# Four graph layers on one TensorE: a hand-written event list made binding for every engine, a first range without Strassen-style products, and counts split in three

## The chip, the cores and the metric

The kernel runs on one core of a Trainium2 chip. The metric is the device time of one launch in microseconds (us), the median of several runs. One launch computes four layers, whose heavy part is seven multiplications of a 2708 x 2708 adjacency matrix with a feature matrix 512 wide, all in float32.

## The reference, cut to what matters

```python
deg = jnp.maximum((adj != 0).astype(jnp.float32).sum(-1), 1.0)
x = _layernorm(x + _L0_gnn_ref(x, adj))      # inc = adj + (adj > 0) / sqrt(count of adj > 0 in the row)
                                             # (inc @ x) / (row sum of inc)
x = _layernorm(x + _L1_gnn_ref(x, adj, adj, ...))   # adj @ x, then an attention-weighted adj @ (x @ W_sa)
x = _layernorm(x + _L2_gnn_ref(x, adj, weight))     # three hops: p = adj @ p, each through a 512 x 512 weight
x = _layernorm(x + _L3_gnn_ref(x, adj, deg[..., None], W, b))
```

Layer 0 needs, for every row of adj, the number of positive entries (the "count") before its product can start, and the sum of the row of inc afterwards. Layer 1 needs two sweeps over adj (one plain, one with attention weights in place of adj), layer 2 three sweeps, layer 3 one.

## The kernel before, in words

**Sweeps and ranges.** Each of the seven multiplications is a sweep, S[0] to S[6], over four ranges of output rows (`RANGES`, L29: 384, 384, 256 and 330 rows of each half; sweep 0 takes them in the order 256, 384, 384, 330, `RANGES0`, L30). The matrix is cut into halves of NH = 1354: A11, A12, A21, A22 against B11, B12, B21, B22. A range is computed with seven products instead of eight, in the manner of Strassen and Winograd: sums of A tiles (s1 to s4, function `comb`, L246, issued at L269 to L272) and of B tiles (T1 to T4, function `x_sums`, L152) are formed on DVE (VectorE), seven products P1 to P7 run on PE (TensorE, L283), and the results are put together from PSUM (`copy_out` on ACT, L304, and `add` on DVE, L311). A product is 11 row tiles (13 in sweeps 3 to 5) by two column blocks. The profile counts two records per float32 matmul, so that one product of an 11-tile sweep shows 44.

**The event list.** Nothing is written in the order of execution. Every step is put on a list by `at(position, function)` (L115). A position is counted in products: a range is 7 long, a sweep 28. At the end the list is sorted and run (L807). So `at(pb + 6.08, ...)` means "when product 6 of this range has just begun". The functions issue instructions to the framework, which adds the semaphores, gives out buffers and orders the instructions of each engine itself: with a cost model it takes, for every engine, the first instruction in list order that it thinks ready. An instruction later in the list can so be put ahead of an earlier one.

**Buffers.** The tiles of A, the temporaries of sweep 0 ("s") and of sweep 2 ("e", "f"), the loads for counting ("cl"), the rows and running sums share one ring of `RING` = 44 buffers of 128 x 384. `NTMP` = 12 temporaries hold products on their way out, `nat` has 7 tiles of 128 x 512, masks have 3 buffers. All eight PSUM banks share one tag.

**Queues.** A tiles, count tiles and re-read features go through SP's DMA queue (`load` L240, L408, `fetch` L386). B tiles go through POOL's (`x_load` L177), except those that ACT's queue loads at the start. Weights go through ACT's.

**Around the change.**
- *Counts* (sweep 0). `count_tile` (L402) does three things in one event: it loads a tile of adj (L408), makes a 0/1 mask with two ACT instructions, Sign and Relu (L410, L411), and multiplies the mask by a column of ones on PE (L416). `count_row` (L419) turns counts into count^-0.5 (DVE, then POOL's power), spreads it over partitions with PE transposes (L434), and ACT copies it into `row` (L437). For the first range the counts of half 0 use the tiles of A that are loaded anyway; those of half 1 load A21 and A22 a second time as "cl".
- *prep0* (L446). For each tile of A in sweep 0, DVE forms mask times row (L449), adds it (L450), and adds the tile to a running row sum (`add_run`, L444). *prep2* (L634) does the like for the attention weights of sweep 2. `run_sums` (L453) reduces the running sums on PE. Both halves are reduced at position 4.5 of a range.
- *done* functions (L328 to L333) take the finished rows of half 1 at position 6.08 and of half 0 at 7.06, three tiles each: transposes or dense products on PE, a layernorm (L336: DVE statistics, POOL's power at L343, DVE's last step at L345), stores.
- *Order of products*: `PLAIN` (L31) is P1, P7, P5, P6, P2, P4, P3. `FIRST` (L32) is that of the first range of sweep 0. P2 uses A12 against B21; P4 uses A22; P3 uses s4, which `comb` writes over A12.
- *next_x* (L179) loads the B tiles of the next sweep while the last range of this one still runs.

Of the kernel before, what the change touches and what calls it, by code (L numbers as in the profile page):

```python
# [30 lines left out]
PLAIN = dict(P1=0, P7=1, P5=2, P6=3, P2=4, P4=5, P3=6)  # L31
FIRST = dict(P1=0, P2=1, P7=2, P5=3, P6=4, P4=5, P3=6)  # L32
STAT = dict(P1="B11", P7="T3", P5="T1", P6="T2", P2="B21", P4="T4", P3="B22")
MOV = dict(P1="11", P7="s3", P5="21", P6="11", P2="12", P4="22", P3="12")
RING = 44
NTMP = 12
# [7 lines left out]
def gnn_kernel(ctx: ExitStack, tc: tile.TileContext, x, adjT, w_sa, a_sa, w_gcn, b_gcn, wab, bab, w_hop, w_out,  # L44
# [58 lines left out]
    def nat(nm):  # L103
        return pool.tile([P, D], F32, name=nm, tag="nat", bufs=7)

    def mask_tile():
        return pool.tile([P, 384], BF, name="mask", tag="mask", bufs=3)
# [44 lines left out]
    def x_sums(k):  # L152
        w = wt(k)
        b = b12.pop(k)
        b11, b21, b22 = (X[s, k] for s in ("B11", "B21", "B22"))
        for d, i, j in (("T3", b22, b), ("T1", b, b11), ("T2", b22, "T1"), ("T4", b21, "T2")):
            j = X[j, k] if isinstance(j, str) else j
            nc.vector.tensor_tensor(new_x(d, k)[:w], i[:w], j[:w], ALU.subtract)  # L158

    def b12_tile(k):  # L160
        b12[k] = pool.tile([P, HD], F32, name="b12", tag="b12", bufs=3)
        return b12[k]
# [16 lines left out]
    def next_x(base, src, direct, sums=0.95, halves=0.50):  # L179


        for k in range(KT):
# [3 lines left out]
            if not late:  # L186
                at(base - 5.8 + f, lambda k=k: x_load(src, k, "B11", q))
                at(base - 1.8 + f, lambda k=k: x_load(src, k, "B21", q))
                at(base - 0.8 + f, lambda k=k: x_load(src, k, "B22", q))
                at(base - 0.8 + f, lambda k=k: x_load(src, k, "B12", q))  # L190
                at(base - 0.4 + f, lambda k=k: x_sums(k))
# [23 lines left out]
    def sweep(base, nk, ranges, prep=None, extra=None, done=None, evac=None, ext_src=None, lead=0.0, first=False,  # L215
              late=None):
        A, spare = {}, {}
        for r, (R0, n) in enumerate(ranges):
            pb = base + 7 * r
            ph = FIRST if first and r == 0 else PLAIN  # L220
            ks = range(nk)

            def load(ij, k, R0=R0, n=n, r=r, ph=ph):
                hi, hj = int(ij[0]) - 1, int(ij[1]) - 1
                w = wt(k)
                if ph is FIRST and ij == "22" and k >= KT - 8:
# [19 lines left out]
            def comb(dst, a, b, op, k, n=n, r=r):  # L246
# [3 lines left out]
                nc.vector.tensor_tensor(A[r, dst, k][:w, :n], A[r, a, k][:w, :n], A[r, b, k][:w, :n], op)  # L250

            when = {"11": (-1.0, 1.0), "21": (-0.4, 1.0), "22": (0.5, 1.0), "12": (2.4, 1.0)}
            cw = {"s3": 0.3, "s1": 1.1, "s2": 2.1, "s4": 5.05}
            if ph is FIRST:
                when = {"11": (-4.0, 0.2), "12": (-3.8, 0.2), "21": (-0.3, 0.4), "22": (0.2, 0.4)}
# [590 lines left out]
```

## Time and profile before

| | us |
|---|---|
| median of 3 runs (3285.07 to 3288.18) | 3286.8 |
| the profiled execution | 3290.12 |
| its span, first to last instruction | 3288.3 |
| PE busy / its idle time in the span | 3166.4 / 121.9 |
| DVE, ACT, POOL busy | 1648.1, 567.6, 349.1 |
| first product starts / sweep 1's first product starts | 61.06 / 533.96 |

All times after this come from that profiled execution. "Busy" for PE is a modelled, pipelined time: PE that is busy is not always PE at its peak, so a product's length is best read where products follow each other without a break. "The chain of waits" follows the work that ended last back to what released it. "Waits" lists for an engine how long it stood idle before an instruction and which engine released it. A window gives busy times, the granted TensorE clock and the DMA engines' share for a stretch of the span. DMA-issuing instructions are shown on the queue's own row (SPq, ACTq, POOLq) and are not counted as busy.

### The profile page before, as it was taken

How to read it: one execution, taken by the hardware profiler on the slowest of the kernel's cores; microseconds unless marked ns; L12 is line 12 of the kernel's file. 1: busy time of each engine (PE TensorE's matmuls, PEld its weight loads, DVE VectorE, ACT ScalarE, POOL GpSimd, SP SyncE). 2: the span in 40 equal slices, each digit the busy share in tenths (PEclk: the TensorE clock that was granted, in tenths of full speed). 3: DMA queues.
4: the chain of work that ended last, by engine and by line, in shares of the span. 5: the costliest groups of instructions: out<-in, count | busy, mean ns of one | idle time of the engine just before them, and what ended most of it. 6: DMA issues, size and time to landing. Idle time of an engine off the chain costs nothing.

```text
span 3288.3 us, 35613 instructions
## 1 busy us (share of the span) xinstructions
PE 3166.4 (96%) x12046; PEld 2050.3 (62%) x12046; DVE 1648.1 (50%) x4093; ACT 567.6 (17%) x1126; POOL 349.1 (11%) x604
## 2 busy tenths in 40 slices
PE   3998999999999999999999999999999999999998
PEld 2755566556765555764556865568656587655675
DVE  6687687334346865975223333323244243643444
ACT  4432500000025544641000000000000000000000
POOL 2001023000000010113000010000011011300000
PEclk9999998999999999999999999999999999999999
DMA  6665665422434342553432453324444344533340
GB/s 201 205 145 121 169 97 138 93 70 50 93 81 111 100 134 80 147 163 118 108 98 72 121 159 90 108 71 116 130 128 125 89 142 130 179 112 99 108 128 33
DMA packets 268683, 383.21 MB, mean 117 GB/s; under 512 B 35199, under 2 KB 230071, under 8 KB 268500
## 3 DMA queue, kind: packets, MB, share of 16 engines
q1 hardware_dynamic: 231096, 291.61, 34.0%
q0 software_dynamic: 28688, 78.49, 7.6%
q10 hardware_dynamic: 8716, 10.84, 1.1%
q8 instruction: 95, 1.56, 0.2%
q14 instruction: 88, 0.72, 0.1%
HBM read 325.31 MB, written 55.49 MB: 116 GB/s over the span
## 4 chain that ended last, share of the span: by engine, by line
PE 83%; issue 6%; DVE 4%; DMA 4%; POOL 2%; ACT 0%; SPq 0%; POOLq 0%; ACTq 0%; DVEq 0%
PE accu L283 21%; PE accc L283 20%; PE accd L283 20%; PE acca L283 10%; PE ps_d L381 8%; DMA cl<-in_adjT 1%; PE ps_n L367 1%; POOL B L177 1%; POOL rstd L343 1%; DMA a<-in_adjT 1%; PE ps_t L373 1%; PE pz L606 1%; DVE T L158 0%; DVE run L444 0%; DVE s L449 0%
## 5 line engine op out<-in xcount | busy, mean ns | idle before, releaser
L250 DVE TENSOR_TENSOR a<-a,a 128x384 f32<-128x384 f32 (+4 forms) x988 | 485.0, 507 | 260.1 <-DMA a<-in_adjT 107.8
L283 PE MATMUL accu<-a,B 128*128 128x384 f32 (+5 forms) x1232 | 395.1, 464 | 0.0
L283 PE MATMUL accc<-s,T 128*128 128x384 f32 (+5 forms) x1232 | 373.3, 458 | 3.6 <-DVE s L250 3.6
L283 PE MATMUL accd<-a,B 128*128 128x384 f32 (+5 forms) x1232 | 376.4, 451 | 0.0
L283 PE MATMUL acca<-a,B 128*128 128x384 f32 (+5 forms) x1232 | 367.7, 452 | 0.0
L283 PE MATMUL accd<-a,T 128*128 128x384 f32 (+5 forms) x1232 | 364.2, 453 | 0.3 <-DVE a L250 0.3
L283 PE MATMUL accu<-a,T 128*128 128x384 f32 (+5 forms) x1232 | 360.6, 450 | 0.0
L283 PE MATMUL accc<-a,T 128*128 128x384 f32 (+5 forms) x1200 | 354.5, 452 | 0.0
L250 DVE TENSOR_TENSOR s<-a,a 128x384 f32<-128x384 f32 (+4 forms) x332 | 166.8, 506 | 318.2 <-PE accc L283 263.7
L283 PEld LDWEIGHTS accc<-s,T 128*128 128x128 f32 (+1 forms) x1232 | 233.8, 194 | 115.8 <-issue 6.7
L283 PEld LDWEIGHTS accd<-a,T 128*128 128x128 f32 (+1 forms) x1232 | 233.3, 191 | 114.6 <-issue 2.4
L283 PEld LDWEIGHTS accu<-a,B 128*128 128x128 f32 (+1 forms) x1232 | 233.0, 196 | 111.5 <-issue 23.8
L283 PEld LDWEIGHTS accu<-a,T 128*128 128x128 f32 (+1 forms) x1232 | 231.7, 190 | 110.5
L283 PEld LDWEIGHTS accc<-a,T 128*128 128x128 f32 (+1 forms) x1200 | 226.1, 190 | 112.6 <-ACT W L304 2.2
L283 PEld LDWEIGHTS accd<-a,B 128*128 128x128 f32 (+1 forms) x1232 | 226.5, 190 | 106.2 <-issue 13.5
L283 PEld LDWEIGHTS acca<-a,B 128*128 128x128 f32 (+1 forms) x1232 | 228.6, 190 | 102.9
L311 DVE TENSOR_TENSOR W<-W,accd 128x384 f32<-128x384 f32 (+2 forms) x56 | 28.1, 505 | 313.9 <-PE accd L283 311.7
L311 DVE TENSOR_TENSOR W<-W,U 128x384 f32<-128x384 f32 (+2 forms) x56 | 28.3, 509 | 280.2 <-ACT U L304 279.2
L444 DVE TENSOR_TENSOR run<-run,a 128x384 f32<-128x384 f32 (+5 forms) x328 | 165.2, 505 | 0.6
L343 POOL TENSOR_TENSOR rstd<-rstd,neg_half 128x1 f32<-128x1 f32 (+1 forms) x88 | 54.8, 623 | 1039.8 <-DVE rstd L342 1034.0
L304 ACT COPY U<-accu 128x384 f32<-128x384 f32 (+2 forms) x56 | 24.4, 439 | 584.9 <-PE accu L283 583.7
L641 ACT ACTIVATE e<-row,neg_s 128x384 f32<-128x384 f32 (+4 forms) x176 | 100.8, 573 | 96.5 <-DVE a L644 32.1
(178 smaller groups left out, 2997.6 us busy)
## 6 DMA issues: line engine op xcount, KB each, us to landing
a<-in_adjT SPq DMA_DIRECT2D x560, 192.0 KB
a<-in_adjT SPq DMA_DIRECT2D x280, 165.0 KB
a<-in_adjT SPq DMA_DIRECT2D x273, 128.0 KB
cl<-in_adjT SPq DMA_DIRECT2D x80, 192.0 KB
ld<-X SPq DMA_DIRECT2D x60, 256.0 KB
Y<-y POOLq DMA_DIRECT2D x54, 256.0 KB, 2.3
B<-Y POOLq DMA_DIRECT2D x84, 128.0 KB, 3.4
X<-o POOLq DMA_DIRECT2D x36, 256.0 KB, 3.2
```

What stands on the lines that cost most here:

```text
L177: eng.dma_start(out=t[:w], in_=q)
L250: nc.vector.tensor_tensor(A[r, dst, k][:w, :n], A[r, a, k][:w, :n], A[r, b, k][:w, :n], op)
L283: nc.tensor.matmul(B[home, c][:, :n], X[STAT[p], k][:w, c * P : (c + 1) * P], A[r, MOV[p], k][:w, :n], start=bool(start and k == k0), stop ...
L304: nc.scalar.copy(T[nm, c][:, :n], B[home, c][:, :n])
L311: nc.vector.tensor_tensor(d[:, :n], T[t, c][:, :n], o[:, :n], ALU.add)
L343: nc.gpsimd.tensor_tensor(rstd[:w, 1:2], rstd[:w, 0:1], neg_half[:w], ALU.pow)
L367: nc.tensor.transpose(ps[:w, c * P : (c + 1) * P], C[h, c][:, lo : lo + w], ident)
L373: nc.tensor.transpose(ps[:, c, :w], cols(dsts, c)[:w], ident[:w, :w])
L381: nc.tensor.matmul(ps[:w], lhs(c), wts[c], start=c == 0, stop=c == DC - 1)
L444: nc.vector.tensor_tensor(run[R0, h][:w, :n], run[R0, h][:w, :n], t[:w, :n], ALU.add)
L606: nc.tensor.matmul(pz[:w], C[h, c][:, lo : lo + w], wab_sb[:, c, :], start=c == 0, stop=c == DC - 1)
L641: nc.scalar.activation(e[:w, :n], row[R0, h][0][:w, :n], AF.Exp, bias=neg_s[:w, t : t + 1])
```

## The change

It does the following.

1. After the list has run, every instruction is tied to the one before it on its engine, so that each engine's order is the list's.
2. The first range of sweep 0 is computed as eight plain products (A11·B11 + A12·B21 and so on), one position earlier; it needs no sums of A or B. The B sums for the later ranges are made at position 6.0, T3 in the place of B12. The X tiles come through SP and ACT, in an order of their own.
3. Counts are split into `count_load`, `count_mask` and `count_tile`, half a product and a fifth of a product apart; `count_row` is split from `spread_row`. The first range's counts of half 1 take their masks from the loaded A21 and A22, and the masks of half 0 are made on DVE.
4. P4 comes before P2; s4 is written over A11 instead of A12; half 1 is finished from position 5.15 (before: 6.08), half 0 from 7.12 (before: 7.06).
5. Running row sums take s1 and s4 (22 additions per range) instead of the four tiles (44), except in the plain range; `run_sums` of half 0 first adds half 1's.
6. Layernorms in sweep 0, except the last one, take their last step on ACT.
7. Buffers: ring 46, temporaries 9, `nat` 6, masks 4, `b12` 4. Loads of A22 and A12 come later in a range, B21 of the next sweep later too; in sweep 1 mask and count are two events; in sweep 6 two early loads move with the order of products.

```diff
-PLAIN = dict(P1=0, P7=1, P5=2, P6=3, P2=4, P4=5, P3=6)
-FIRST = dict(P1=0, P2=1, P7=2, P5=3, P6=4, P4=5, P3=6)
+PLAIN = dict(P1=0, P7=1, P5=2, P6=3, P4=4, P2=5, P3=6)
+FIRST = [("11", "B11", "a"), ("12", "B21", "a"), ("11", "B12", "b"), ("12", "B22", "b"),
+         ("21", "B11", "c"), ("22", "B21", "c"), ("21", "B12", "d"), ("22", "B22", "d")]
-RING = 44
-NTMP = 12
+RING = 46
+NTMP = 9
...
-                at(base - 1.8 + f, lambda k=k: x_load(src, k, "B21", q))
-                at(base - 0.8 + f, lambda k=k: x_load(src, k, "B22", q))
-                at(base - 0.8 + f, lambda k=k: x_load(src, k, "B12", q))
-                at(base - 0.4 + f, lambda k=k: x_sums(k))
+                at(base - 0.89 + f, lambda k=k: x_load(src, k, "B21", q))
+                at(base - 0.88 + f, lambda k=k: x_load(src, k, "B22", q))
+                at(base - 0.87 + f, lambda k=k: x_load(src, k, "B12", q))
+                at(base - 0.6 + f, lambda k=k: x_sums(k))
...
+                if sums and (dst, a) in (("21", "21"), ("11", "12")):
+                    add_run(R0, int(dst == "21"), n, w, A[r, dst, k])
-            when = {"11": (-1.0, 1.0), "21": (-0.4, 1.0), "22": (0.5, 1.0), "12": (2.4, 1.0)}
-            cw = {"s3": 0.3, "s1": 1.1, "s2": 2.1, "s4": 5.05}
...
+            when = {"11": (-1.0, 1.0), "21": (-0.4, 1.0), "22": (0.75, 0.8), "12": (3.2, 1.0)}
+            cw = {"s3": 0.3, "s1": 1.25, "s2": 2.1, "s4": 4.3}
+            pw = {ij: (p + 0.3, f) for ij, (p, f) in when.items()}
+            if plain:
+                when = {"11": (-4.0, 0.2), "12": (-3.8, 0.2), "21": (-2.4, 0.4), "22": (-1.6, 0.4)}
+                pw = {"11": (-0.9, 0.6), "12": (-0.3, 0.6), "21": (3.3, 0.9), "22": (4.1, 0.9)}
...
+                for i, (home, h, e) in enumerate((("a", 0, 0), ("b", 0, 1), ("c", 1, 0), ("d", 1, 1))):
+                    at(pb + 2 * i + 2.02, lambda a=(home, h, e), f=whole: f(*a))
...
-                p0 = pb + (6.08 if h else 7.06)
+                p0 = pb + (5.15 if h else 7.12) if not plain else pb + (8.12 if h else 4.15)
...
+        if on_scalar:
+            nc.vector.scalar_tensor_tensor(rstd[:w, 0:1], mv[:w, 0:1], -1.0, rstd[:w, 1:2], ALU.mult, ALU.mult)
         for d, c0, c1 in dsts:
+            if on_scalar:
+                nc.scalar.activation(d[:w], y[:w, c0:c1], AF.Identity, bias=rstd[:w, 0:1], scale=rstd[:w, 1:2])
+                continue
...
+    def count_mask(R0, n, h, i, t=None, on_vector=False):
+        w = wt(i % KT)
+        t = cnt.pop((R0, h, i)) if t is None else t
+        cnt[R0, h, i] = m = mask_tile()
+        if on_vector:
+            nc.vector.tensor_scalar(m[:w, :n], t[:w, :n], 0.0, None, ALU.is_gt)
+        else:
+            nc.scalar.activation(m[:w, :n], t[:w, :n], AF.Sign)
+            nc.scalar.activation(m[:w, :n], m[:w, :n], AF.Relu)
...
+            for h, p, d in ((0, -3.7, 0.05), (1, 1.9, 0.055)):
+                for i in range(NT):
+                    a = lambda h=h, i=i: A[0, f"{h + 1}{i // KT + 1}", i % KT]
+                    at(pb + p + d * (i - 2 * h), lambda h=h, i=i, a=a: count_mask(R0, n, h, i, a(), h == 0))
+                    at(pb + p + d * i, lambda h=h, i=i: count_tile(R0, n, h, i))
...
+                    q = pb + p + 2.5 * i / NT
+                    at(q - 0.5, lambda i=i, h=h: count_load(R1, n1, h, i))
+                    at(q - 0.2, lambda i=i, h=h: count_mask(R1, n1, h, i))
+                    at(q, lambda i=i, h=h: count_tile(R1, n1, h, i))
...
-        for h in range(2):
-            at(pb + 4.5 + 0.05 * h, lambda h=h: run_sums(R0, n, h, inverse))
+        at(pb + (5.6 if r else 3.3), lambda: run_sums(R0, n, 0, inverse, r > 0))
+        at(pb + (2.6 if r else 6.4), lambda: run_sums(R0, n, 1, inverse, r > 0))
...
     for k in range(KT):
         f = k / KT
-        at(-3.0 + f, lambda k=k: x_load(X0, k, "B11", nc.scalar))
-        at(-0.8 + f, lambda k=k: x_load(X0, k, "B21", nc.gpsimd))
-        at(-0.2 + f, lambda k=k: x_load(X0, k, "B22", nc.gpsimd))
-        at(0.0 + f, lambda k=k: x_load(X0, k, "B12", nc.gpsimd))
-        at(0.6 + f, lambda k=k: x_sums(k))
-    at(4.0, start0)
+        at(-5.0 + f, lambda k=k: x0_load(k, "B11"))
+        at(-4.5 + 0.3 * f, lambda k=k: x0_load(k, "B21"))
+        at(-4.0 + 0.3 * f, lambda k=k: x0_load(k, "B12"))
+        at(-3.0 + 0.3 * f, lambda k=k: x0_load(k, "B22"))
+        at(6.0 + 0.9 * f, lambda k=k: x_sums(k))
+    at(2.6, start0)
...
-        for ij, p in (("11", -0.6), ("21", 0.05), ("22", 0.9), ("12", 4.1)):
+        for ij, p in (("11", -0.6), ("21", 0.05), ("22", 1.05), ("12", 3.6)):
             for k in range(KT):
                 at(pb + p + 0.8 * k / KT, lambda ij=ij, k=k: go(ij, k))
+                at(pb + p + 0.8 * k / KT + 0.12, lambda ij=ij, k=k: tally(ij, k))
...
-        early = {(1, 2): -2.0, (1, 3): -1.9, (0, 0): -2.0, (0, 1): -1.9}
+        early = {(1, 2): -0.95, (1, 3): -0.9, (0, 0): -1.0, (0, 1): -0.95}
...
     for _, _, fn in sorted(events, key=lambda e: e[:2]):
         fn()
+
+    last = {}
+    for i in nc.cur_bb.bb.instructions:
+        if i.engine in last:
+            tc.add_manual_dep(i, last[i.engine].name,
+                              mybir.DependencyInfo(mybir.DependencyClass.NoSync, mybir.DependencyReason.DATA),
+                              reason="order of the list")
+        last[i.engine] = i
```

In the diff `plain` is true for the first range of sweep 0, where `pb` is -1; `start0`, which loads the attention weights of layer 1 and reduces them on DVE, moves from 4.0 to 2.6.

## The prediction

> **What bounds the kernel now.** I read the page's parts 1 and 2, then PE's waits, then windows cut at the ranges of sweep 0.
>
> ```profile
> PE 3166.4 (96%) x12046; PEld 2050.3 (62%) x12046; DVE 1648.1 (50%) x4093; ACT 567.6 (17%) x1126; POOL 349.1 (11%) x604
> ...
> PE   3998999999999999999999999999999999999998
> ```
>
> PE is the bound: it stands idle for 121.9 us only, and the slices put about half of that in the first 82 us. The rest must be seen in windows (sweep 0's ranges start at 61.06, 151.40, 283.47 and 423.01):
>
> ```profile
> 0.00:61.06 61.06, 10.56 (x93) 6.57 (x93) 29.37 (x92) 31.32 (x90) 20.30 (x41) 1.00 0.85 258
> 61.06:151.40 90.34, 83.71 (x480) 68.78 (x480) 64.59 (x197) 43.51 (x98) 4.59 (x6) 0.96 0.55 165
> 151.40:283.47 132.07, 124.17 (x527) 74.27 (x527) 104.00 (x264) 47.82 (x101) 12.07 (x19) 0.93 0.64 162
> 283.47:423.01 139.54, 125.67 (x555) 76.24 (x554) 105.22 (x273) 45.62 (x102) 17.76 (x29) 0.95 0.60 132
> 423.01:533.96 110.95, 103.63 (x442) 73.24 (x441) 95.69 (x275) 6.12 (x12) 28.48 (x51) 0.95 0.68 140
> ```
>
> The columns are length, then busy us of PE, PEld, DVE, ACT, POOL, then clock, DMA share, GB/s. Before 61.06 PE works 10.6 us, while the DMA engines are 0.85 busy. In the four ranges the clock is 0.93 to 0.96 (1.00 in nearly all of what follows) and DVE is busy 72 to 86% of the time. Who holds PE:
>
> ```profile
> PE cnt L416 <- ACT mask L411: 46.3, 25, 9.3
> ...
> PE ps_t L373 <- DVE o L345: 21.3, 6, 6.4
> PE pr L434 <- POOL r L431: 5.6, 6, 1.2
> ```
>
> The first line is for 0 to 61, the others for 61 to 600. PE waits for the masks of the counts, in front of a product whose operands are ready: it executes its queue in order, and the counts of half 1 stand ahead of P1. Later it waits for layernorms that are late on DVE. After 600 its waits sum to only 17 us, 9.1 of them for the last `add` (U, L311).
>
> **PE's own work.** Without a break, a product takes:
>
> ```profile
> 585.81 14.19 PE accd L283 x44
> ...
> 838.71 9.50 PE accd L283 x44
> ...
> 934.28 12.21 PE accd L283 x44
> ```
>
> for 384, 256 and 330 rows. Beside products: from 356.44 to 372.44 one product with 11 count groups took 16.0, so (16.0-14.19)/11 = 0.17 a group of three; a finished tile 0.44+0.44+0.81 = 1.7 (transposes, transposes, the small product, spacings at 412 to 420); sums and row spreads about 2 a range. Range 1: 99.3 + 44 x 0.17 + 6 x 1.7 + 2 = 118.9. It took 132.1: 13.2 lost. Range 2, likewise: 20.6. Range 3: 85.5+10.2+2.5 = 98.2, 12.8 lost. Range 0 has 66.5+7.5+6.8+1.5 = 82.3, 8.0 lost. Sum 54.6, and 50 before the start.
>
> **The start.** Loads before the first count of range 1 (list position 0.0): X 5.55 MB and range 0 of A 5.55 MB. The 2.8 MB of A21 and A22 read twice for counts are gone. From 2 to 26 us the window shows 298 GB/s at a DMA share of 0.95: 11.1 MB take 37 us, to 39. Then a count tile, a mask (2 x 0.42) and PE: 42. At that point the first product is over (its masks, 22 x 0.29 on DVE, and its rows are ready near 23; preparation is 2 x 0.336 a tile against PE's 0.86). The other end is SP's own issue:
>
> ```profile
> 0.74 17.66 SPq L240 DMA_DIRECT2D a<-in_adjT  x22
> ```
>
> 0.80 each; 77 of them take 62 us, so 64 instead of 42. I take 42, since SP, in a calmer stretch (44.11, two in 0.86), issued one in 0.43. X leaves POOL's queue; POOL has nothing else then. The Trainium skill ("DMA: Bandwidth & Descriptors", "Rules for kernel authors") says that spreading DMAs over SP, ACT and GpSimd brings no bandwidth and saves issue time only; by it, moving X to SP costs nothing up to SP's limit. This change tests that.
>
> **Range 0, plain.** From 0.0: the seven products that remain after the first one (7 x 9.5 = 66.5; the seven of before cost the same, so the added eighth is the one that runs before 42, beside the loads), range 1's counts 7.5, half 1's own counts 2.6 (22 groups of two at 0.12), two finished tiles of half 0 3.4, sums and row spreads 1.5: 81.5. ACT is short here: between positions -0.2 and 2.3 it makes 22 masks of 0.84 and 22 of 0.61 and two copies, 32.6 us, while PE needs 19.6+5.6 = 25.2 for that stretch: +7.4. `start0` waits on its weights, but ACT issues them some 7 us before DVE's next tile is due: 0 (3 if not). Range 1 so starts at 42+81.5+7.4 = 131, against 151.4. DVE saves the 44 sums of A in this range and makes its 44 x_sums at 6.0 instead of before the start (44 x 0.336 = 14.8 us); PE's last two products cover them, and without that cover they would stand before range 1's preparation.
>
> **Ranges 1 to 3.** `add_run` falls from 44 to 22 (22 x 0.47 = 10.3 us of DVE; in sweep 2 too, where PE doesn't wait for it: 0). P4 before P2 lets half 1 be finished at 5.15, and this takes its three layernorms out of the crowded place around 7. What is left there: from 7.02 to the third layernorm, 30 instructions of 0.47 and three layernorms of 3.4 (0.67+0.60+0.12+0.07, POOL's wait 1.8, 0.15), 24.3 us; PE reaches the third transposes 20.4 after the same point: 4 lost a range, 6 in the first (x_sums beside it). The 1.8 is this row, between the statistics and L345:
>
> ```profile
> 308.42 0.55 DVE L345 TENSOR_SCALAR o<-ld,mv,rstd 128x512 f32<-128x512 f32 x1 [1.31 <-POOL rstd L343]
> ```
>
> The last step on ACT has no row; ACT with one scale pointer took 0.72 (L613, 128x512), a bias pointer adds at most 0.13 (L641 0.611 against L304 0.478): 0.72 to 0.85, taken 0.85, against 0.55 on DVE. So the chain to PE gets 0.4 longer and DVE 0.4 shorter. By the skill ("ScalarE: Activation LUTs", "What ACT_TABLE_LOAD costs"), 280 + 0.833 ns per element and 93 for a second pointer, it would be 0.80; the rule speaks against the move, the sum stays within 0.1 us a tile. **New wait:** `run_sums` at 5.6 stands right behind DVE's added addition, which stands behind a layernorm from 5.45: PE waits 1.3 to 2, and products queue behind it. Counts in three steps take off POOL's 5.6 and the mask waits of 5.5: a mask is due 0.2 of a product (2.8 us) before its count, and a count row 0.15 (2.1 us) before its spread, against a chain of 1.75 (last count at 25.18, transposes at 26.94). So ranges 1 to 3: 126, 124, 103 (now 132.1, 139.5, 111.0). Sweep 1 starts at 131+126+124+103 = 484 instead of 534: **-50**.
>
> **Sweeps 1 to 6.** No arithmetic changes on PE. P4 before P2 frees A22 a product earlier and moves half 1's finish under P2; half 0's transposes get 0.06 of a product more (0.9 us): of the 9.1 us of waits for U I give 5 back. B21 is loaded behind P2, 0.3 of a product (4 us) before x_sums, against 3.4 us to landing on POOL's queue; T1 is needed two products later: 0. Smaller pools (9, 6): lifetimes fit, 0. Masks apart from counts in sweep 1: -1. A binding order costs something unknown: nothing if the old order was near the list's, at most about 1 us in each of 24 ranges from rows like `ps_d <- xT` (0.5): 0 to 24, I take 4, the near end, because DVE and ACT are idle over half of these sweeps. The tail behind the last product is unchanged. Net **-2**.
>
> **Sum.** 3290.1 - 52 = 3238 for a profiled execution; that stands 3.3 above the median of before, so 3235 as a median. What a measurement of this kernel tells from no change is about 0.2%, 6.6 us.
>
> **Rivals.**
> 1. *Only the start gains.* Ranges 1 to 3 keep their 46.6 us, because DVE's list still has prep, sums and layernorms in one place. For it: DVE 79, 75 and 86% busy. Against: 10 us less of DVE each, and less at 7. -20 or (SP-bound, half) -10: about 3270.
> 2. *The binding order makes PE slower.* Place: the three or so tiles around 7.1 to 8.2 of every range. A list counted in products knows nothing of transfers and layernorms; one late DMA on SP or a POOL round trip on DVE stops all behind it, and nothing may pass. Price: the 4 us that I find in sweep 0, in the other 24 ranges, 96: 3286.8-52+96 = 3331. It decides from 2.2 us a range. For it: DVE stands 1.8 us in each layernorm, SP waits 639 us for buffers behind `accc`. Against: PE has only 17 us of waits in those sweeps now, and outside sweep 2 the slices show DVE 20 to 60% busy, so a late step there is caught up before PE needs the next one.
> 3. *The order changes nothing* in sweeps 1 to 6, because the framework followed the list already. The time is the forecast's; only the cause differs, so it has no chance of its own; a version with the list order alone, or without it, would tell.
> 4. *More than forecast:* ranges 1 to 3 at PE's floor, ACT no hindrance: -80, 3206.
>
> **Chances.** Forecast (3206 to 3270) 0.62, rival 1 (to 3280) 0.14, below 3206 0.05; within 0.2% 0.04; slower 0.15, rival 2. Faster 0.81. The range 3206 to 3290 leaves out rival 2 and the lowest case, 0.20, and takes in SP's issue end (+22) and the order's (+20).
>
> **What would show it.** First product near 23 to 30, second near 42 (64: SP bound). Range 1 starts near 131; ACT masks lead PE's waits between 42 and 75. `add_run` (L444) with some 180 to 190 records instead of 328. Granted clock in ranges 1 to 3 above 0.96. `ps_t <- DVE`/ACT at most 5 us a range. Sweep 1's first product near 484, and from there to the end the same 2754 us within 15. Wrong if PE's waits after sweep 0 grow beyond 40, or sweep 1 starts after 515.

## The result, and the profile after

The changed kernel takes 3402.8 us (median of 4 runs, 3401.7 to 3405.7), the kernel before 3287.5 (median of 4): a ratio of 1.035, with an interval of 1.0334 to 1.0370. It is slower by 115 us where 52 us less were forecast, and lies above the range and above rival 2's 3331 too. The profiled execution has a span of 3401.5.

The page's parts 1 and 2 of the changed kernel (busy us of each engine; 40 slices of 85 us in tenths, with the granted clock in the last line):

```profile
PE 3201.7 (94%) x12090; PEld 2064.8 (61%) x12090; DVE 1607.5 (47%) x3914; ACT 548.2 (16%) x1092; POOL 323.3 (10%) x571
...
PE   5878986999999899999899999999999999999998
...
PEclk8989998999999999999999999999999999999999
```

PE's idle time has grown from 121.9 to 199.8 us, and its busy time from 3166 to 3202. An eighth product of 9.5 us is in that; the rest goes with a lower clock, in the mean of the span 0.976 instead of 0.987. The first slice is better than before in busy time (5 for 3); slices 2, 3, 6, 7, 14 and 20 are worse, and slices 1 and 3 have a lower clock. Slices 14 and 20 lie in sweep 2 and in sweep 3's first range.

Where that is, the windows cut at the ranges of sweep 0 tell (the columns as before: length, busy us of PE, PEld, DVE, ACT, POOL, clock, DMA share, GB/s):

```profile
0.00:26.48 26.48, 5.38 (x47) 3.18 (x47) 7.81 (x31) 1.66 (x2) 1.43 (x7) 1.00 0.73 213
26.48:161.20 134.72, 100.70 (x577) 81.26 (x578) 76.97 (x221) 63.97 (x146) 7.06 (x11) 0.89 0.60 159
161.20:308.50 147.30, 125.82 (x539) 74.41 (x538) 108.02 (x262) 54.03 (x108) 12.99 (x22) 0.93 0.57 133
308.50:450.10 141.60, 129.67 (x556) 77.93 (x555) 99.92 (x254) 50.60 (x108) 15.58 (x26) 0.94 0.60 127
450.10:595.90 145.80, 110.71 (x439) 75.03 (x437) 94.69 (x258) 7.96 (x15) 30.61 (x56) 0.87 0.61 121
```

The start gained 34.6 us (61.1 to 26.5). Then the four ranges lost 44, 15, 2 and 35, so that sweep 1 starts at 595.9 instead of 534.0. From there on, sweep 1 is 5 shorter, sweep 2 is 57 longer (555.5 for 498.8), sweeps 3 to 5 are together 9 shorter and sweep 6 is 9 longer.

What PE waits for, over the whole span of the changed kernel:

```profile
PE cnt L459 <- ACT mask L449: 45.8, 23, 14.4
PE deg L653 <- DVE mask L641: 28.2, 6, 13.9
PE cnt L459 <- DVE mask L446: 18.1, 18, 3.8
```

Before, all such waits sum to 108 us, now to 188. No single releaser stands out: masks of counts (L446, L449), the masks of sweep 1 (L641), transposed tiles (L407, 13.1), layernorms, running sums. Four places can be read in full.

**Range 0.** In the changed kernel's timeline, ACT's first mask for the next range:

```profile
52.12 0.52 ACT L448 ACTIVATE mask<-cl 128x384 bf16<-128x384 f32 x1 [26.62 <-DMA cl<-in_adjT]
```

PE at the same time:

```profile
53.26 0.24 PE L459 MATMUL cnt<-ones_bf,mask 128*128 128x1 bf16 x3 [14.35 <-ACT mask L449]
```

And SP's queue ahead of it:

```profile
43.35 4.11 SPq L245 DMA_DIRECT2D aw<-in_adjT  x8
47.97 13.37 SPq L438 DMA_DIRECT2D cl<-in_adjT  x18
```

The first product is over at 38.9 (its last group starts at 29.63 and takes 9.27). PE then stands 14.35 us before a count of range 1, though the second product's operands lie ready (DVE prepares the last of its A tiles until 43.1), since the count's tile is issued by SP at 47.97 only, behind all of range 0's tiles and X.

The second longest wait of this range, 7.91 us, is made by the fixed order on ACT. A mask stands there behind the last step of a layernorm (part 6 of the change), which waits for DVE:

```profile
116.83 0.81 ACT L375 ACTIVATE o<-ld,rstd 128x512 f32<-128x512 f32 x1 [12.80 <-DVE rstd L372]
118.67 0.24 PE L459 MATMUL cnt<-ones_bf,mask 128*128 128x1 bf16 x3 [7.91 <-ACT mask L449]
```

In e3 below, where ACT alone is free, masks go ahead of that step, and PE's waits for them behind the second product are at most 1.85 us.

**The end of sweep 0.** DVE in the timeline of the changed kernel:

```profile
573.38 0.43 DVE L161 TENSOR_TENSOR T<-b,B 128x256 f32<-128x256 f32 x1 [12.25 <-DMA b<-X]
```

PE there:

```profile
575.39 0.24 PE L653 MATMUL deg<-ones_bf,mask 128*128 128x1 bf16 x3 [13.87 <-DVE mask L641]
575.49 2.55 PE L288 MATMUL accd<-a,B 128*128 128x330 f32 x4
```

POOL there:

```profile
571.17 0.54 POOL L181 DMA_DIRECT2D B<-X  x1 [5.63 <-DMA SR<-rcol]
```

DVE stands 12.25 us before x_sums of one B tile. The masks of sweep 1 (L641, 574.98) are next in its list, so PE's degree count (13.87) and behind it the rest of P3 stand as well; P3, by the code, holds the B22 buffers that POOL's next loads need, and those loads stand behind small stores of rcol. Further rounds follow (5.13 and 2.79 at DVE, 6.85 and 2.08 at PE). PE's idle time in this range is 35.1 us; before it was 7.3.

**Sweep 2, a product at DVE's pace.** PE's timeline of the changed kernel in P5 of the first range:

```profile
1117.52 1.56 PE L288 MATMUL accd<-a,T 128*128 128x384 f32 x4 [0.56 <-DVE a L255]
1124.52 1.44 PE L508 MATMUL rs<-ones_f,run 128*128 128x1 f32 x6 [5.44 <-DVE run L491]
1125.83 7.09 PE L288 MATMUL accd<-a,T 128*128 128x384 f32 x16
```

DVE's, just before that wait ends:

```profile
1119.04 0.55 DVE L255 TENSOR_TENSOR a<-a,a 128x384 f32<-128x384 f32 x1
1119.62 0.56 DVE L491 TENSOR_TENSOR run<-run,a 128x384 f32<-128x384 f32 x1
1120.10 0.55 DVE L715 TENSOR_TENSOR e<-e,f 74x384 f32<-74x384 f32 x1
1120.74 0.56 DVE L716 SCALAR_TENSOR_TENSOR a<-a,e 74x384 f32<-74x384 f32 x1
```

Per tile DVE makes four instructions in a row (weight, weight, s1, running sum), 2.12 us, while PE uses a tile of P5 up in 1.29. PE's groups of four start 2.12 apart (1115.40, 1117.52); then it waits 5.44 before the reduction of the sum, with four tiles of P5 behind it. P5 takes 25.0 us from its first matmul to its last; before it took 14.9, with 0.64 of P6 in between.

**Sweep 2, the border of two ranges.** PE's transposes wait for a layernorm, as rival 2 has it, in P7 of the second range, which takes 34.1 us from start to start (25.8 in e1 below):

```profile
1248.67 1.11 PE L405 MATMUL ps_t<-ident,ld 128*128 128x128 f32 x4 [2.58 <-DVE ld L377]
```

### The profile page after: what moved, and what is told of

Same layout as the page of the kernel before. It is cut to its first block, busy times and chain, and to the rows that moved or that the text cites. A ratio compares the mean times of both kernels' runs of the same rounds, so it can differ in the third digit from the quotient of the medians.

```text
span 3401.5 us, 35466 instructions
## 1 busy us (share of the span) xinstructions
PE 3201.7 (94%) x12090; PEld 2064.8 (61%) x12090; DVE 1607.5 (47%) x3914; ACT 548.2 (16%) x1092; POOL 323.3 (10%) x571
## 4 chain that ended last, share of the span: by engine, by line
PE 47%; issue 12%; DVE 3%; DMA 2%; POOL 1%; ACT 0%; SPq 0%; ACTq 0%; POOLq 0%; DVEq 0%
PE accu L288 12%; PE accd L288 11%; PE accc L288 11%; PE acca L288 6%; PE ps_d L413 6%; DMA x3T<-X3T 1%; DMA b<-Y 1%; PE ps_n L399 1%; DVE a L255 0%; PE ps_t L405 0%; DVE run L491 0%; DVE e L715 0%; POOL B L181 0%; POOL Y L389 0%; DMA b<-X 0%
## 5 line engine op out<-in xcount | busy, mean ns | idle before, releaser
L255 DVE TENSOR_TENSOR a<-a,a 128x384 f32<-128x384 f32 (+5 forms) x963 | 433.8, 505 | 118.1 <-DMA a<-in_adjT 117.8
L288 PE MATMUL accu<-a,B 128*128 128x384 f32 (+5 forms) x1188 | 379.9, 466 | 1.3 <-DVE a L497 1.3
L288 PE MATMUL accd<-a,B 128*128 128x384 f32 (+5 forms) x1188 | 359.1, 457 | 0.0
L288 PE MATMUL accu<-a,T 128*128 128x384 f32 (+5 forms) x1188 | 349.7, 452 | 0.0
L288 PEld LDWEIGHTS accu<-a,B 128*128 128x128 f32 (+1 forms) x1188 | 224.4, 195 | 113.2 <-issue 22.5
L288 PEld LDWEIGHTS accc<-s,T 128*128 128x128 f32 (+1 forms) x1188 | 225.5, 195 | 110.6 <-issue 10.0
L288 PEld LDWEIGHTS accu<-a,T 128*128 128x128 f32 (+1 forms) x1188 | 223.5, 190 | 109.6
L288 PEld LDWEIGHTS acca<-a,B 128*128 128x128 f32 (+1 forms) x1188 | 221.0, 190 | 109.9 <-issue 14.9
L255 DVE TENSOR_TENSOR s<-a,a 128x384 f32<-128x384 f32 (+4 forms) x321 | 146.7, 505 | 0.0
L715 DVE TENSOR_TENSOR e<-e,f 128x384 f32<-128x384 f32 (+5 forms) x176 | 88.8, 505 | 43.8 <-ACT f L714 43.7
L389 POOL DMA_DIRECT2D Y<-y x57 | 31.1, 545 | 812.1 <-ACT y L791 750.0
```

Source lines behind the costliest of these rows:

```text
L288: nc.tensor.matmul(B[home, c][:, :n], X[STAT[p], k][:w, c * P : (c + 1) * P], A[r, MOV[p], k][:w, :n], start=bool(start and k == k0), stop ...
L389: nc.gpsimd.dma_start(out=dst[:, c0:c1], in_=d[:w])
L715: nc.vector.tensor_tensor(e[:w, :n], e[:w, :n], f[:w, :n], ALU.min)
```

## The experiments

All edits are to the changed kernel unless it is said otherwise. The kernel before was run beside each group; its medians in the groups were 3287.6 to 3300.9, so a ratio is the safer comparison between groups, and some microseconds of a difference are chance. The first four runs undo the tie of part 1 for all engines, or for one.

### e1: no order tied

```diff
-    last = {}
-    for i in nc.cur_bb.bb.instructions:
-        if i.engine in last:
-            tc.add_manual_dep(i, last[i.engine].name,
...
```

> The changed kernel without the ties between instructions: the framework orders each engine again, all other edits stay. Theory (the binding order makes engines stand behind one late step: DVE behind B tiles at the end of sweep 0, ACT behind copies in sweep 2): 3250 to 3310, of the 115 us lost nearly all come back; sweep 2 takes 500 us again instead of 555, sweep 0 ends before 540. Rival (the list's new positions, the swap of P4 and P2 and the smaller pools cost it, whoever orders): 3380 to 3410, sweep 2 still near 550.

Measured: 3263.6, ratio 0.9889 [0.9873, 0.9906]. Sweep 1 starts at 529.9, sweep 2 is 507.2 long. The rest of the change, then, gains 1.1%, and the tie of the order costs the changed kernel 1.0352/0.9889, 4.7%, or 139 us by the two medians: part 1 alone explains the sign.

It shows too how freely the framework reorders. The first product starts at 56.5 here instead of 26.5. DVE's timeline of e1:

```profile
50.87 4.57 DVE L161 TENSOR_TENSOR T<-B,T 128x256 f32<-128x256 f32 x13 [6.11 <-DMA B<-in_x]
55.37 0.75 DVE L496 SCALAR_TENSOR_TENSOR s<-a,row 128x256 f32<-128x256 f32 x2
```

And the wait that PE has from it, among e1's waits:

```profile
PE acca L298 <- DVE a L497: 26.1, 1, 26.1
```

x_sums of list position 6.0 stand on DVE ahead of the preparation of position -1.9, and wait there for transfers of X. PE waits 26.1 us for that, in one wait, and still sweep 1 starts 4 us earlier than before the change.

### e2, e3, e4: all tied but DVE, ACT or SP

```diff
     for i in nc.cur_bb.bb.instructions:
+        if i.engine.name in ('DVE',): continue
```

(for e3 `'Activation'`, for e4 `'SP'`).

> The changed kernel with every engine bound but DVE. Theory: DVE's fixed place is the larger part of the loss, since the longest new waits of PE (28 us for deg masks, 10 for run_sums, 25 for C, U and layernorms) end with DVE: 3310 to 3340, the 13.9 us wait before the deg count at the end of sweep 0 gone, sweep 2 near 520. Rival (ACT or SP is the one that blocks): 3390 to 3410.

> The changed kernel with every engine bound but ACT. Theory: ACT's place matters in sweep 2 (exponentials stand behind the copy of U for 13 us) and in range 0 (masks behind copies): 3360 to 3385, sweep 2 near 535, sweep 0 unchanged at its end. Rival (ACT is only where DVE's and the ring's lateness shows): 3395 to 3405.

> The changed kernel with every engine bound but SP, whose DMA queue the framework orders again. Theory: SP follows the releases of buffers by DVE and ACT, so little changes: 3385 to 3410; the count tiles of range 1 still land after all of range 0's loads, first count of range 1 near 53 us. Rival (transfers held behind others on SP are the cause): under 3350 and that count before 45.

Measured: 3323.0, ratio 1.0070 [1.0052, 1.0088]; 3385.6, 1.0259 [1.0241, 1.0276]; 3398.4, 1.0298 [1.0279, 1.0318]. Against the changed kernel's 3402.8 that is 80, 17 and 4 us, by the ratios 2.8, 0.9 and 0.5%: DVE matters, ACT a little, SP hardly. e2 is as its theory has it. e3's theory fails on the place: sweep 2 is 558.1 long with ACT free, no shorter than the 555.5 with all tied. In e4 the first count of range 1 starts at 51.4, so SP's list order is not what makes it late.

SP's order has a price in one place all the same, the last three ranges of sweep 6. They take 338 to 340 us in every run here in which SP is tied to the end, and 328 to 329 in every one in which it isn't (328.7 in e4, 329.6 before). In the changed kernel PE waits 7.8 us in sweep 6 for the additions of L852 (and DVE 34 for the loads of x3T ahead of them), in e4 0.7 (and under 1). These are 10 of the 139 us; sweep 6's first range gives 3 back.

### e6: DVE alone tied; e10: all but PE

```diff
     for i in nc.cur_bb.bb.instructions:
+        if i.engine.name != 'DVE':
+            continue
```

(for e10 the reverse, with `'PE'` left out.)

> The changed kernel with DVE's order tied to the list and every other engine's left to the framework. e2 (all tied but DVE) was 80 us faster than the changed kernel, e1 (none tied) 139 us. Theory A (DVE's order costs by itself: DVE stands in waits for transfers and for ACT, with work that PE needs behind it): e1 plus 60 to 80, so 3325 to 3345, ratio near 1.01; sweep 1 starts 40 later than in e1. Rival B (DVE's order costs only together with that of PE and POOL, in a circle in which each waits for the next): within 20 of e1, at most 3284.

> The changed kernel with every engine's order tied to the list but PE's. Theory A (PE's order is what turns the lateness of the others into lost time): near e6, 3270 to 3300, ratio at most 1.004; PE takes P4 ahead of P5 in sweep 2, whose length falls below 525, and sweep 1 starts before 545. Rival B (DVE, ACT, POOL and SP in order make the operands late for whatever PE picks): 3340 or more, and PE's idle time grows instead of its order changing.

Measured: e6 3273.0, ratio 0.9953 [0.9937, 0.9970]; e10 3323.3, ratio 1.0108 [1.0093, 1.0124]. For e6 rival B holds: the engine that gives 80 us when it is freed (2.8% by the ratio) costs only 9 when it is tied alone (0.6% by the ratio, or some 21 us). e10's time lies between its two cases; sweep 2 is below 525 and sweep 1 starts before 545, as theory A has it. How PE uses its freedom can be seen in e10's timeline, in the same P5:

```profile
1066.23 1.56 PE L288 MATMUL accd<-a,T 128*128 128x384 f32 x4 [0.15 <-DVE a L255]
1067.63 1.45 PE L288 MATMUL accc<-a,T 128*128 128x384 f32 x4
1068.92 1.45 PE L288 MATMUL accd<-a,T 128*128 128x384 f32 x4
```

`accd<-a,T` is P5, `accc<-a,T` is P4: matmuls of a product that is two places later fill the time in which DVE makes the next s1, and PE hardly stands.

### e9, e13, e14: pairs and threes

```diff
     for i in nc.cur_bb.bb.instructions:
+        if i.engine.name not in ('DVE', 'PE'):
+            continue
```

(for e13 with `'Pool'` added, for e14 with `'Activation'`.)

> The changed kernel with the orders of PE and DVE tied to the list, those of ACT, POOL and SP left to the framework. DVE alone cost 17 us over e1 (e6), everything but DVE 59 (e2), all five 139. Theory A (the loss is PE in its order behind DVE in its order: PE may not take a product whose operands are ready while it waits for a mask or a sum that DVE makes late): at least 80 of the 139 are here, 3345 to 3400, ratio 1.02 to 1.035, and sweep 2 is near 550 long as in the changed kernel (507 in e1, 517 in e6). Rival B (it takes the queues as well: POOL's and SP's transfers in order close the circle): 3280 to 3310, sweep 2 below 525.

> The changed kernel with PE, DVE and POOL tied to the list, ACT and SP left to the framework. PE and DVE alone (e9) start sweep 1 at 560.9 and are 35 us faster at that point than all five tied. Theory A (POOL's loads of the next B tiles close the circle at the end of sweep 0: load, x_sums, masks, count, last product, next load): sweep 1 starts at 580 to 596, time 3375 to 3400. Rival B (the rest is ACT's and SP's): sweep 1 starts within 8 of 561, time within 12 of e9's 3356.

> The changed kernel with PE, DVE and ACT tied to the list, POOL and SP left to the framework. Theory A of e13 (POOL): sweep 1 starts within 8 of e9's 560.9, time within 12 of 3356. Rival B (ACT's masks in list order hold PE's counts in the first and the last range of sweep 0): sweep 1 starts at 580 to 596, time 3375 to 3400, and PE's waits for ACT's masks are 40 or more, as in the changed kernel (45.8; e9 35.5).

Measured: e9 3355.9, e13 3364.1, e14 3372.1. With the other runs of this kind, by the profiled spans (us) and the ratio to the kernel before:

| tied | sweep 1 starts | sweep 2 long | ratio |
|---|---|---|---|
| none (e1) | 529.9 | 507.2 | 0.9889 |
| DVE (e6) | 523.2 | 516.8 | 0.9953 |
| all but DVE (e2) | 551.9 | 522.5 | 1.0070 |
| all but PE (e10) | 540.7 | 517.3 | 1.0108 |
| PE, DVE (e9) | 560.9 | 558.3 | 1.0217 [1.0198, 1.0237] |
| PE, DVE, POOL (e13) | 569.6 | 560.8 | 1.0232 [1.0217, 1.0248] |
| PE, DVE, ACT (e14) | 588.3 | 554.7 | 1.0253 [1.0239, 1.0267] |
| all but ACT (e3) | 581.9 | 558.1 | 1.0259 |
| all but SP (e4) | 603.6 | 554.8 | 1.0298 |
| all | 595.9 | 555.5 | 1.0352 |

In sweep 2 the matter is settled, and e9's theory A with it. Tying DVE adds 10 us, tying all the others adds 15; PE and DVE together add 51, as much as all five (48). The loss belongs to the pair: DVE in its order makes an operand late, PE in its order may take no other.

The first column is less sharp: in e15 below, whose code is the same up to sweep 2, sweep 1 started 8.0 later than in the changed kernel, so differences below some 10 us say nothing there. e9's row is from the shortest of its four runs (3347.2; the others are 7 to 17 us longer). The pair takes sweep 1's start from 530 to 561. POOL's 9 on top of that (e13) is within the scatter; the time agrees with its rival B, whose bound for the start (within 8) is missed by less than 1; ACT's 27 (e14) is not, and puts the start where rival B had it, though the whole time is 3 below B's range and the waits for ACT's masks are 35.0 where B wanted 40. Freeing ACT alone from all five (e3) gives back only 14. So the shares of single engines don't add up, and I give none beyond the pair's and SP's 10 in sweep 6. PE alone was not tied.

### e5 and e11: the order tied only at the start

```diff
-    for _, _, fn in sorted(events, key=lambda e: e[:2]):
+    bound = None
+    for p, _, fn in sorted(events, key=lambda e: e[:2]):
+        if bound is None and p >= 1.0:
+            bound = len(nc.cur_bb.bb.instructions)
...
-    for i in nc.cur_bb.bb.instructions:
+    for i in list(nc.cur_bb.bb.instructions)[:bound]:
```

(e11: `p >= 7.0`, and the counts of e7 below.)

> The changed kernel, but only the instructions of list positions below 1.0 (the start and the first two plain products) are tied to the one before them on their engine; everything after is left to the framework's own order, as in e1. In e1 the first product started at 56.5, with all tied at 26.5. Theory A (the list's order is worth its 30 us at the start and costs only later): first product at 26 to 28, sweep 1 starts near 510 instead of e1's 530, time 3240 to 3250, ratio to before near 0.982. Rival B (the early product gains nothing, because the counts of the next range and their loads are as late as ever and PE waits for them in any case, as it does for 14.35 us in the changed kernel): first product at 26, second range starts where e1's does, 156 within 5, time 3264 within 6.

> The changed kernel with all engines tied only for list positions below 7 (sweep 0's first range and the loads before it), the rest left to the framework, and with the counts of the second range later within the first, as in e7. Theory A (the list's order is right where it was laid out by hand, the start, and costs elsewhere): the first product at 25 to 31, range 1 starts near 140 (e7: 139.3), the other ranges as in e5 (127, 129, 114), sweep 1 starts near 510, time 3235 to 3245, ratio 0.982 to 0.987. Rival B (what range 0 gains, the framework's order loses again at its border, where instructions of later positions may still be put ahead on every engine): sweep 1 starts after 522, time 3250 or more, no better than e5.

Measured: e5 3256.2, ratio 0.9897 [0.9882, 0.9911]; e11 3252.3, ratio 0.9894 [0.9879, 0.9909]. Neither of e5's two cases came: the first product starts at 54.4, because the untied x_sums of position 6.0 are still put ahead of the tied preparation on DVE (x_sums at 48.74 after a wait of 5.13 for X, the first preparation at 53.23). e11 starts at 27.7 and its range 1 at 142.1, as theory A has it, but this range then takes 140.5 (e5: 127.1), so sweep 1 starts at 525.1, rival B's case. These three (e1, e5, e11) can't be told apart, and all beat the kernel before by 1.0 to 1.1%: a first product 30 us earlier is worth nothing by the end of range 1.

### e7: the next range's counts later in the first range

```diff
-            for h, p in ((0, 1.0), (1, 3.8)):
+            for h, p, g in ((0, 3.3, 2.0), (1, 5.4, 2.0)) if r == 0 else ((0, 1.0, 2.5), (1, 3.8, 2.5)):
...
-                    q = pb + p + 2.5 * i / NT
+                    q = pb + p + g * i / NT
```

> The changed kernel, all engines tied, with the next range's counts (load, mask, count, row) put later within the first range alone: half 0 from position 3.3 over 2.0 products instead of from 1.0 over 2.5, half 1 from 5.4 over 2.0 instead of from 3.8 over 2.5. Theory A (the first range lost its 44 us to an early count in front of the second product and to ACT's masks): the 14.35 us wait ahead of the second product goes, range 1 starts near 140 instead of 161, time 3403 - 20 = 3383, ratio 1.029. Rival B (range 0 is bound by the transfers of its own A21 and A22 tiles or by ACT, wherever the counts stand): range 1 starts within 5 of 161, time within 8 of 3403.

Measured: 3379.2, ratio 1.0276 [1.0261, 1.0292], 24 us less than the changed kernel; range 1 starts at 139.3 instead of 161.2. Theory A holds. PE's waits for ACT's masks in the first range fall from 30.4 to 10.5, as e7's waits up to 140 us show:

```profile
PE cnt L459 <- ACT mask L449: 10.5, 3, 8.9
```

### e8: x_sums 0.2 of a product later

```diff
-                at(base - 0.6 + f, lambda k=k: x_sums(k))
+                at(base - 0.4 + f, lambda k=k: x_sums(k))
```

> The changed kernel, all engines tied, with one number back where it was before: the next sweep's x_sums at its base - 0.4 instead of base - 0.6 (0.2 of a product, 2.4 us, later for every tile). Theory A (at the end of sweep 0 DVE stands in x_sums for a B tile that is still on its way; masks, counts, PE's last product and POOL's next load stand behind it in a circle, so each tile pays the transfer): sweep 1 starts some 20 us earlier than 595.9, the DVE wait of 12.25 us shrinks, and the ends of sweeps 1 to 5 gain 0 to 3 us each, time 3375 to 3385, ratio near 1.028. Rival B (the B tiles are late because the DMA engines are full there, share 1.05, and would be as late for x_sums anywhere): sweep 1 starts within 6 of 595.9, time within 8 of 3403.

Measured: 3387.2, ratio 1.0290 [1.0272, 1.0309]. The time is 2 us above theory A's, and its reason doesn't hold. (The profile is of the longest of e8's four runs, 3396.0.) DVE still waits 11.79 us there, in e8's timeline:

```profile
577.46 0.43 DVE L161 TENSOR_TENSOR T<-b,B 128x256 f32<-128x256 f32 x1 [11.79 <-DMA b<-X]
```

Sweep 1 starts 9.6 earlier, no more than the scatter; its first range is 12.9 longer, and at its second range (732.2 against 728.9) nothing is left. What was gained stands at the border of sweeps 2 and 3: sweep 3's first range takes 147.0 instead of 156.8. So the lateness at the end of sweep 0 is not x_sums' place in the list alone. No later place was tried.

### e12: the order of products alone, on the kernel before

```diff
-PLAIN = dict(P1=0, P7=1, P5=2, P6=3, P2=4, P4=5, P3=6)
+PLAIN = dict(P1=0, P7=1, P5=2, P6=3, P4=4, P2=5, P3=6)
...
-                at(pb + cw["s4"] + f, lambda k=k, comb=comb: comb("12", "12", "11", ALU.subtract, k))
+                at(pb + cw["s4"] + f, lambda k=k, comb=comb: comb("11", "12", "11", ALU.subtract, k))
...
-                p0 = pb + (6.08 if h else 7.06)
+                p0 = pb + ((6.08 if h else 7.06) if ph is FIRST else (5.15 if h else 7.12))
```

> The kernel before with one part of the change alone and nothing tied: P4 ahead of P2 in every range but sweep 0's first, s4 written over A11, half 1 finished from 5.15 and half 0 from 7.12, the loads of A22 and A12 and the sums at the changed kernel's positions, and sweep 6's two early loads. Theory A (the 1.1% by which e1 beats the kernel before is this order): time 3262 to 3272, ratio near 0.993; sweep 2 with the first range of sweep 3 takes 649 (before 657, e1 648), each first range of sweeps 4 and 5 some 3 less, PE's waits for layernorms in sweep 0 fall from 21.3 to below 8 and sweep 1 starts near 522. Rival B (the gain is in the start, the counts and the running sums): ratio 0.998 to 1.002, sweep 1 starts within 5 of 534.

Measured: 3291.1, ratio 1.0010 [1.0001, 1.0018]. By the time this is rival B, though not by sweep 1's start. In the parts, theory A is right outside sweep 0 and wrong in it: sweep 2 with sweep 3's first range takes 649.5, that range 141.1 instead of 158.3 (as in e1), the first ranges of sweeps 4 and 5 are 2.9 and 2.2 shorter; but sweep 1 starts at 556.9, 23 later. Finishing half 1 at 5.15 puts its layernorms where the counts are, and the waits for layernorms stay while those for masks rise. Of e12's waits between 140 and 560 us:

```profile
PE ps_t L373 <- DVE o L345: 20.5, 7, 4.7
PE cnt L416 <- ACT mask L411: 12.4, 4, 5.2
PE pr L434 <- POOL r L431: 7.9, 4, 6.3
```

In e1, where counts come in three steps, additions are halved and the layernorms' last step is on ACT, sweep 1 starts at 529.9 with the same order. Before, these three lines were 21.3, 4.2 and 3.8. So the parts need each other: the order of products gains 22 once sweep 1 has begun and costs 23 in sweep 0, and the other parts take 27 off sweep 0.

### e15: sweep 2's running sums later

```diff
+                if sums and base == S[2]:
+                    at(pb + 2.2 + f, lambda k=k, R0=R0, n=n, r=r: add_run(R0, 1, n, wt(k), A[r, "21", k]))
...
-        at(pb + 2.6, lambda: run_sums(R0, n, 1, share))
+        at(pb + 3.6, lambda: run_sums(R0, n, 1, share))
```

> The changed kernel, all engines tied, with one edit in sweep 2 alone: the additions of s1 into the running sum stand in events of their own from position 2.2 of a range instead of right behind each s1 from 1.25, and half 1's running sum is reduced at 3.6 instead of 2.6. Theory A (P5 runs at DVE's pace, since prep 0.58 + 0.48, s1 0.58 and addition 0.48 make 2.12 us a tile against PE's 1.29, and then PE waits for the reduction): without the addition a tile is 1.5 us, P5 of the first range takes 16 to 19 instead of 25.0, the 5.44 us wait goes, sweep 2 is 25 to 40 shorter than 555.5, time 3363 to 3378, ratio near 1.023. Rival B (DVE has no slack in sweep 2 when its order is fixed, so the additions only make P6, P4 or P2 late instead): sweep 2 within 8 of 555, time within 10 of 3403.

Measured: 3397.3, ratio 1.0299 [1.0282, 1.0316]; sweep 2 is 540.2 long. The sweep is between the two cases, the time in rival B's; the time gained less than the sweep, since sweep 2 began 9.7 later. In the first range theory A is right to the letter (P5 14.2 instead of 25.0, the wait gone, the range 11.8 shorter), in the other three the loss has another place: 2.6, 1.0 and 0 come back. There P7 is the long one (34.1 from start to start in the second range of the changed kernel, 31.6 in e15, 25.8 in e1), with the layernorm wait shown above.

The list order by itself, on the old code, wasn't tried.

## Why the prediction was wrong

The step that failed is "A binding order costs something unknown: [...] 0 to 24, I take 4". It costs 139 us (e1). The bound came from the wrong row: a wait of 0.5 that the trace of before shows is what is left after the framework has reordered, and says nothing of what the reordering saves. The rows that bore on it were there: DVE's per-tile chains in sweep 2, and the transfers of B at a sweep's end. "Nothing if the old order was near the list's" was a condition that could have been looked into: the order of DVE's instructions in the trace of before against their list positions. Rival 3, that the order changes nothing, is refuted by the same run.

By steps:

- *Start.* First product near 23 to 30: 26.5. Right. Second at 42, or 64 if SP's issue binds: 53.4. SP issued 77 tiles in 47.2 us without a pause (0.61 each, between the 0.43 and the 0.80 that I had), the DMA engines were busy at 0.73 in the first 26 us, where I had taken 0.95. So I read the queue and not the bandwidth as the limit; no run loads X elsewhere. X on SP's queue put its 17.5 us of issue ahead of the count tiles. The rule of the Trainium skill that spreading loads over queues saves issue time alone ("DMA: Bandwidth & Descriptors", "Rules for kernel authors") agrees with this reading.
- *Range 0.* 131 was forecast as range 1's start; 161.2. ACT's masks hold PE for 30.4 us in this range, but 14.35 of them are the late count tile and 7.91 the layernorm on ACT, neither of them in the term for ACT. The 8 that are left are of the size of the ACT shortage of 7.4, in part by luck: the 0.84 taken for a mask of 384 columns is twice the 0.42 of one with 256, and the trace of before has 0.97 (masks at 201.54 and 202.50). `start0`, put at 0, cost something too: DVE stands 5.68 us before it, since ACT issues its weights from 92.86 on only, behind masks. e7, where the counts move, gives 139.3, 8 above the forecast.
- *Ranges 1 to 3.* 126, 124 and 103 forecast; 147, 142 and 146. Without the tie, e5 has 127, 129 and 114: the first forecast is right, the last 11 too low; an 11.3 us wait for sweep 1's masks (L641) ahead of the border, a place that I hadn't priced, is as long. Also wrong: the clock, said to be above 0.96, is 0.93, 0.94 and 0.87. Right: L491 has 182 records (180 to 190 forecast). The layernorm's last step on ACT takes 0.813 us (16 records, the first three ranges; the fourth keeps it on DVE); 0.85 was taken. The estimate of 0.80 from the Trainium skill ("ScalarE: Activation LUTs", "What ACT_TABLE_LOAD costs") was nearer. `ps_t` waits 8.3 us for this step in range 1, where at most 5 were forecast.
- *"In sweep 2 too, where PE doesn't wait for it: 0".* Half the additions are gone there, but those left stand in s1's path. e15 shows that their place costs 15 us of the 57.
- *Sweeps 1 to 6, the order of products.* Forecast 5 us from the waits for U; e12 and e1 gain 22 and 20 after sweep 1's start. Sweep 3's first range is 17 shorter in both, of which a longer sweep 2 takes 8 to 10 back, since half 1's work of sweep 2 is done there instead of in sweep 3. Sweep 1's first range is 8 shorter, those of sweeps 4 and 5 some 2 to 3 each. The sign was right, the place and the size others.
- *"Wrong if PE's waits after sweep 0 grow beyond 40, or sweep 1 starts after 515."* They grew from 17 to 65, and it starts at 595.9; from there to the end it takes 2806 us instead of 2754.

Rival 2 had the mechanism and the sign, at 0.15, and not the size or the place. It put 4 us on the finished tiles at every border. Against e1, 66 of the 137 us between the two spans are lost before sweep 1, 48 in sweep 2, 16 in sweep 3's first range and 8 in sweep 6; the other borders of sweeps 1 and 3 to 5 lose next to nothing, as its "against" had it. In sweep 2, P7 behind a border is 8.3, 9.3 and 4.2 us longer and not 4, and P2 is 3 to 5 longer in every range. It also took the cost as that of single waits: e6, e9 and e10 show that it is made by two queues, each in a fixed order.

Open: what the loss at the end of sweep 0 consists of. The circle of load, x_sums, mask, count, product and next load can be read in the trace; e8 moved one member of it, and POOL's order, which is free in e9 and tied in e13, changes that range only from 134.1 to 135.9 (145.8 with all tied, 116.6 in e1).

## What to carry to other kernels

Waits in a trace are those that a scheduler has left over; they don't bound what its reordering saves. Before an order is fixed, compare for every engine the instruction order of the trace with the list, and price a fixed order by pairs of engines: an operand that is late on one costs only if the consumer may take nothing else. Measure the code without the tie as well: here the rest of the change was worth 1.1%, and a tie of the first stretch alone (e5, e11) could not be told from none.

## What the runs showed of the hardware

**A wait of more than some 3 us costs more than its length, through the clock.** Windows of 1 us around the 5.44 us wait in sweep 2 (PE stands from 1119.1 to 1124.5; the clock is the column before the DMA share):

```profile
1122.00:1123.00 1.00, 0.00 (x0) 0.00 (x0) 0.97 (x3) 0.00 (x0) 0.00 (x0) 0.71 0.67 143
1123.00:1124.00 1.00, 0.00 (x0) 0.00 (x0) 0.97 (x3) 0.00 (x0) 0.00 (x0) 0.50 0.15 54
...
1128.00:1129.00 1.00, 1.00 (x3) 0.56 (x2) 0.86 (x7) 0.69 (x2) 0.00 (x0) 0.50 0.55 127
1129.00:1130.00 1.00, 1.00 (x4) 0.57 (x3) 0.93 (x6) 0.39 (x1) 0.00 (x0) 0.88 0.19 69
```

The clock falls to a half some 3.3 us into the wait and comes back 4.7 us after work resumes. The 16 matmuls from 1125.83 on take 7.09 us, where 16 at full clock take 5.33 (at 1107.80); at the end of sweep 0, after the waits of 13.87, 6.85 and 2.08, four matmuls take 2.55 that take 1.36 otherwise. The Trainium skill ("TensorE: Matmul & The Clock Gate", "What's actually happening") has at least one window of about 3.4 us for both ways; the trace agrees with 3.3 and 4.7. So 32 us of PE's idle time in sweep 2 (e1: 0.2) became 48 us of length: half of the waits' sum again is paid in slow matmuls that are counted as busy (523.6 us at a mean clock of 0.97, in e1 507.0 at 1.00). In e10 no wait of that sweep is over 1.7 us; they sum to 7.6, and the clock stays at 1.00.
